# Fast matrix products for the keys and values of a linear attention, and a re-ordered beginning and end, in a four-layer hybrid kernel on one core

## The chip, the core and the metric

The kernel runs on one core of one Trainium2 chip. A core has a matmul engine (TensorE, PE in the profile; its weight loads are shown apart as PEld), VectorE (DVE), ScalarE (ACT), GpSimd (POOL) and SyncE (SP), each with its own in-order queue of instructions, and DMA queues that are fed by some of them. Data lie in HBM, are brought to SBUF (128 partitions), and matmul results land in PSUM banks of 128 x 512 f32. The metric is device time in microseconds for one execution.

## What is computed

The input x has 8 batches of 512 tokens with 256 features, all in f32. Four layers follow each other, each on the layer-normed x and added to x:

```python
x = x + linear_attention(layernorm(x))    # "a" in the names
x = x + ffn(layernorm(x))                 # "f"
x = x + attention(layernorm(x))           # "n", 16 heads of 64
x = x + ffn(layernorm(x))                 # "g", the same weights as "f"
```

The linear attention, whose keys and values the change is about, is

```python
Q = l2norm(x @ W_q.T); K = l2norm(x @ W_k.T); V = x @ W_v.T
global_feat = sum over tokens of (K * V) / 512
return Q * global_feat
```

The feed-forward layer mixes each token with the one before it (`xr = mu_r*x + (1-mu_r)*x_prev`, `xk` likewise), and returns `sigmoid(xr @ W_r.T) * (relu(xk @ W_k.T)**2 @ W_v.T)`. The softmax of the attention runs over the query axis.

## The kernel before

**The work.** Batches go through the layers in a software pipeline. The attention is done in 64 pairs of heads (8 batches x 8 pairs, numbered g). Two pairs at a time make one period: scores (`sc`, L1095), a row maximum on VectorE (`nm`, L1100), exponentials on ScalarE (`e`, L1111), values scaled by the sums' reciprocals on GpSimd (`vs`, L1128), and context (`cx`, L1148). Everything else (the linear attention and feed-forward layer of later batches, projections, the output projection `y`, the last feed-forward of earlier batches) is put between these blocks as filling.

**The order.** It is written out when the program is built. Each piece of filling is a generator that yields steps (engine, cost, earliest start), and a small planner (`Order`) keeps a clock for each engine, picks the next step by due time and readiness, and emits it. `until` runs what is due, `fill` adds more up to a share of TensorE's time that `total` hands out evenly. A table `CHOICES` has one entry for each period: an addition to the share, a slack, and a number that shuffles the ranks. On the chip each engine runs its instructions in just that order, and waits on semaphores.

**Seven products.** The head projections, the attention's values from the second batch on and the feed-forward keys from the third batch on are computed as 2 x 2 block matrices with seven products in place of eight (`seven`). It needs sums of weight blocks (made once, `sums_of_weights`), sums of row blocks (made for each batch on GpSimd; `sums_of_rows`, and in `keys` for the feed-forward), and additions behind the products: `begin` copies the first product out of PSUM, `join` and further additions on VectorE combine the rest (L883, L893, L903). Products 1 and 2 share a PSUM bank, 7 and 4, and 5 and 3: the second of each can begin when the result of the first has been used. The products are emitted in the order 1, 6, 7, 2, 5, 4, 3.

**The linear attention** (`linear`): for each half of a batch (256 tokens) the rows are normalized and transposed (the first three batches with TensorE, `normed_t`; the others by a DMA transpose, `normed_dma`). Then for each tile of 128 tokens two matmuls with 512 columns give keys and values together in a bank (L672); ScalarE copies the values out (L678) and sums the squared keys (L679), VectorE multiplies both (L683), and after the inverse norm (`power`, GpSimd) adds the tiles up with the norm as a factor (L692, L694). `mean` sums over tokens with one matmul, `queries` and `front` do the rest and go on to the feed-forward layer.

**The beginning.** Weights and the x of the first two batches are asked for at the start, then `al`. The first two batches' fronts are planned until the second is due (`order.until(-1)`), and after it come the loads of the third and fourth batch and the third one's front. SP's queue holds these loads in the order of the code.

**The end.** The last batch's last feed-forward runs by halves: four matmuls for the output of a half (L440, `o_g`), one multiplication (L569) and one addition (L618) of 128x512 on VectorE, and one store of 256 KB (L1052).

Buffers: `sums`, the row sums of the feed-forward keys, is one tile for each of two sets of buffers (`buffers(own)`, named sumsFalse and sumsTrue); `cpool` holds the contexts of 8 pairs.

Of the kernel before, what the change touches and what calls it, by code (L numbers as in the profile page):

```python
# [8 lines left out]
F32 = mybir.dt.float32  # L9
U16 = mybir.dt.uint16  # L10
AF = mybir.ActivationFunctionType
# [19 lines left out]
PAIRS, BANKS = 3, 2  # L31
X_LANDS = (4.1, 8.5, 12.0)
# [6 lines left out]
    (-4, 2, 90203), (0, 0, 43155), (0, 2, 0), (-2, 2, 77416), (1, 0, 8249), (-2, 1, 93964),  # L39
    (0, 0, 0), (-6, 1, 43070), (-2, 0, 51517), (-2, 2, 70093), (-2, 2, 81842), (-1, 2, 0),  # L40
    (1, 0, 13647), (6, 0, 84141), (1, 0, 16079), (4, 1, 90125), (-6, 0, 25271), (0, -1, 56854),
    (-2, 2, 47130), (0, -1, 47424), (0, 1, 8929), (4, 0, 14836), (-6, 0, 64258), (4, 2, 13478),
    (-1, 1, 84848), (2, 2, 74886), (1, 2, 58853), (4, 2, 96692), (6, 0, 82127), (4, 0, 41997),
    (0, 0, 0), (-1, -1, 26368), (6, 0, 83164), (0, 0, 0),
# [192 lines left out]
def kernel(ctx: ExitStack, tc: tile.TileContext, a: dict, out: bass.AP):  # L237
# [21 lines left out]
    cpool = ctx.enter_context(tc.tile_pool(name="cpool", bufs=8))  # L259
# [70 lines left out]
    def buffers(own):  # L330

        if own not in sets:
            s = {
                n: one.tile([P, 2, 512], F32, tag=f"{n}{own}", name=f"{n}{own}")
                for n in ("xn", "xr", "xk")
            }

            s["ka"], s["r"] = s["xn"], s["xk"]
            s["sums"] = one.tile([P, 3, HS], F32, tag=f"sums{own}", name=f"sums{own}")
            sets[own] = s  # L340
        return sets[own]

    def buffers_linear(b):

        if b < 2:
            return buffers(b == 1)
        if "linear" not in sets:
            n = {n: one.tile([P, 2, 512], F32, tag=f"{n}l", name=f"{n}l") for n in ("xn", "xr")}  # L350
            sets["linear"] = {"xn": n["xn"], "xk": n["xn"], "ka": n["xn"], "xr": n["xr"], "r": n["xr"]}
        return sets["linear"]

# [8 lines left out]
    def normed(src, name, s, h, ready, early=False):  # L362
# [7 lines left out]
        xn, rstd = tiles(s["xn"], h), small.tile([P, 2], F32, tag="rstd", name=f"rstd_{name}_{h}")  # L370
        if early:

            ready = yield "G", 1.05, ready
            nc.gpsimd.tensor_scalar(rstd, mv[:, :, 1], LN_EPS, 1.0, ALU.add, ALU.mult)
            nc.gpsimd.tensor_tensor(rstd, rstd, neg_half[:, :2], ALU.pow)
            ready = yield "V", 0.75, ready
            for u in range(2):
                nc.vector.tensor_scalar(
                    xn[:, u, :], src[:, 2 * h + u, :], mv[:, u, 0:1], rstd[:, u : u + 1],
                    ALU.subtract, ALU.mult,  # L380
                )
        else:

            shift = small.tile([P, 2], F32, tag="shift", name=f"shift_{name}_{h}")
            ready = yield "G", 1.4, ready
            nc.gpsimd.tensor_scalar(shift, mv[:, :, 0], -1.0, None, ALU.mult)
            nc.gpsimd.tensor_scalar(rstd, mv[:, :, 1], LN_EPS, 1.0, ALU.add, ALU.mult)
            nc.gpsimd.tensor_tensor(rstd, rstd, neg_half[:, :2], ALU.pow)
            nc.gpsimd.tensor_tensor(shift, shift, rstd, ALU.mult)
            ready = yield "A", 1.0, ready  # L390
            for u in range(2):
                nc.scalar.activation(
                    xn[:, u, :], src[:, 2 * h + u, :], AF.Identity,
                    bias=shift[:, u : u + 1], scale=rstd[:, u : u + 1],
                )
# [136 lines left out]
    def ffn(xb, name, s, h, ready, add_on, by_dma, due):  # L532
# [32 lines left out]
        order.give()  # L565
        ready = yield "T", BANK, squared, -1, mark
# [5 lines left out]

    def keys(name, s, ready):
# [3 lines left out]
        t = s["sums"]  # L577
        yield "G", 0.0, 0.0, -1, "sums_f"
        for dst, x0, x1 in (
            (t[:, 1, :], b22, b12), (b12, b12, b11), (t[:, 0, :], b22, b12),  # L580
            (t[:, 2, :], b21, t[:, 0, :]),
        ):
            ready = yield "G", 0.8, ready
            nc.gpsimd.tensor_tensor(dst, x0, x1, ALU.subtract)
        order.marks[name, "t"] = ready
        lhs = blocks_of_weights(fk, blocks["sums_f"], split_pairs, 0)
        rhs = [b11, b21, b22, t[:, 2, :], b12, t[:, 0, :], t[:, 1, :]]
# [18 lines left out]
        def through(h, ready):  # L606
            for f in (AF.Relu, AF.Square):
# [43 lines left out]
    def linear(b, h):  # L651
# [3 lines left out]
        xt, kv = chunks(s["xr"], h), tiles(s["ka"], h)  # L655
# [9 lines left out]
        order.marks[f"a{b}", h] = ready  # L665
        ss = small.tile([P, 2], F32, tag="ss", name=f"ssk_{b}_{h}")
        arrived = ready
        for u in range(2):
# [8 lines left out]
            vs = two.tile([P, D], F32, tag="av", name=f"av_{b}_{h}_{u}")  # L677
            nc.scalar.copy(vs, ps[:, D:])  # L678
            nc.scalar.activation(kv[:, u, :], ps[:, :D], AF.Square, accum_out=ss[:, u : u + 1])  # L679
            if u == 1:  # L680
                order.add(queries(b, h), *due_of(b))
            ready = yield "V", 0.35, ready
            nc.vector.tensor_mul(kv[:, u, :], ps[:, :D], vs)  # L683
            order.give()
        rn = small.tile([P, 2], F32, tag="rn", name=f"rnk_{b}_{h}")
# [11 lines left out]
        if both(f"a{b}"):  # L697
            order.add(mean(b, ready), *due_of(b))

# [94 lines left out]
    }  # L794
    blocks["sums_f"] = const.tile([P, 4, P], F32, tag="sums_f", name="sums_f")
# [243 lines left out]
    def tail(b, h, ready, due):  # L1039
# [9 lines left out]
        )  # L1049
        ts = slice(2 * h, 2 * h + 2)  # L1050
# [136 lines left out]
    add_front(1)  # L1187
    order.until(-1)
    al = weight("al", [P, NP, D], nc.sync)
    load_x(2)  # L1190
    load_x(3)
    add_front(2)
# [21 lines left out]
    total += 2 * FAST - 13 * FAST / 2  # L1214
# [76 lines left out]
```

## Time and profile before

| | |
|---|---|
| median of 3 runs | 1146.74 us (1146.02 to 1146.79) |
| the profiled execution | 1146.73 us, its span 1144.8 us |
| TensorE busy | 1125.2 us, 6994 records |
| VectorE, ScalarE, GpSimd busy | 806.0, 679.5, 478.9 us |
| granted TensorE clock | 1.0 |

A line of the profile's groups has the source line, engine, operation, output and inputs by the program's names, the shape (for a matmul partitions x columns of the weights, then the output), the count, then the busy time and the mean duration of one in nanoseconds, then idle time before it. Each f32 matmul shows as two records. Matmuls are pipelined, and a record's end is modelled: the mean of one is longer than the distance to the next.

```profile
L1111 ACT ACTIVATE e<-sc,nm 128x512 f32<-128x512 f32 x512 | 347.1, 690 | 123.1 <-DVE nm L1100 123.1
L1100 DVE TENSOR_REDUCE nm<-sc 128x2 f32<-128x1024 f32 x256 | 308.9, 1218 | 69.3 <-PE sc L1095 68.6
L672 PE MATMUL kv<-wkv,xrl 128*128 128x512 f32 x96 | 44.9, 595 | 0.0
L931 PE MATMUL m_qk<-xta,aq 128*128 128x256 f32 x124 | 38.8, 394 | 0.0
```

The third line is the work that the change rewrites: the keys and values of six batches, 48 matmuls of 512 columns. The fourth is one of the block products that the kernel already has, with 256 columns.

### The profile page before, as it was taken

Reading aid. Unit: us, or ns where it says so; the run is one execution under the profiler, and the core shown is the slowest. Engines: PE = TensorE matmul, PEld = TensorE weight load, DVE = VectorE, ACT = ScalarE, POOL = GpSimd, SP = SyncE. Lnnn points to the kernel's source line nnn. Section 1 sums busy time; section 2 is a strip of 40 time slices with the busy share of each in tenths; the row PEclk is TensorE's granted clock in tenths of the full one; section 3 lists DMA queues with packets and bytes.
Section 4 is the critical chain, followed back from the end, with each engine's and each line's share of the span. In section 5 each row is a group of like instructions: output and inputs, shape, how many; then the busy total and the mean of one; then the engine's idle time right before and its main releaser. Section 6 shows DMA issues by size and latency. Waiting matters only on the chain. (4 is left out here: it accounts for less than half of the span.)

```text
span 1144.8 us, 19233 instructions
## 1 busy us (share of the span) xinstructions
PE 1125.2 (98%) x6994; PEld 699.2 (61%) x6994; DVE 806.0 (70%) x1474; ACT 679.5 (59%) x1789; POOL 478.9 (42%) x760
## 2 busy tenths in 40 slices
PE   7999999999999999999999999999999999999998
PEld 4645456656556567666656555766656756665556
DVE  5775777667777767767677777777677777667754
ACT  3546756467663864655655676466574566645653
POOL 4455263224712484217542267343553442523201
PEclk9999999999999999999999999999999999999999
DMA  8000000000001110012100111010200110001001
GB/s 298 1 1 1 1 19 19 10 11 11 19 11 38 29 28 10 10 37 38 20 10 11 37 32 25 10 47 10 29 19 1 22 35 2 19 19 20 1 2 37
DMA packets 61182, 28.64 MB, mean 25 GB/s; under 512 B 51456, under 2 KB 59648, under 8 KB 60576
## 3 DMA queue, kind: packets, MB, share of 16 engines
q1 hardware_dynamic: 59936, 25.70, 9.2%
q8 instruction: 56, 0.92, 0.3%
q10 hardware_dynamic: 864, 1.05, 0.3%
q0 software_dynamic: 288, 0.67, 0.2%
q14 instruction: 38, 0.31, 0.1%
HBM read 10.63 MB, written 4.19 MB: 13 GB/s over the span
## 5 line engine op out<-in xcount | busy, mean ns | idle before, releaser
L1111 ACT ACTIVATE e<-sc,nm 128x512 f32<-128x512 f32 x512 | 347.1, 690 | 123.1 <-DVE nm L1100 123.1
L1100 DVE TENSOR_REDUCE nm<-sc 128x2 f32<-128x1024 f32 x256 | 308.9, 1218 | 69.3 <-PE sc L1095 68.6
L1095 PE MATMUL sc<-qk 64*64 64x512 f32 x2048 | 270.1, 594 | 2.6 <-DVE qk L903 1.7
L1148 PE MATMUL cx<-e,vs 64*64 64x512 f32 x2048 | 269.1, 589 | 0.0
L1128 POOL TENSOR_TENSOR vs<-v,rs 128x256 f32<-128x256 f32 x128 | 79.0, 618 | 381.8 <-DVE rs L1124 353.6
L1148 PEld LDWEIGHTS cx<-e,vs 64*64 64x64 f32 x2048 | 87.2, 133 | 136.9 <-issue 114.5
L1095 PEld LDWEIGHTS sc<-qk 64*64 64x64 f32 x2048 | 76.1, 132 | 138.9 <-issue 86.8
L440 PE MATMUL y<-al,ctx 128*128 128x256 f32 x512 | 116.4, 380 | 0.4 <-ACT prev_f L517 0.4
L440 PEld LDWEIGHTS y<-al,ctx 128*128 128x128 f32 x512 | 96.6, 190 | 17.5 <-ACT e L1111 3.2
L1111 ACT ACTIVATION_READ_ACCUMULATOR e<-sc,nm 128x1 f32 x512 | 105.3, 206 | 0.0
L939 ACT ACTIVATE qk<-m_qk,bias 128x256 f32<-128x256 f32 x124 | 52.2, 475 | 51.7 <-PE m_qk L931 50.1
L1156 DVE TENSOR_TENSOR ctx<-cx,ctx 128x512 f32<-128x512 f32 x64 | 44.3, 692 | 47.3 <-ACT ctx L1155 46.3
L947 DVE SCALAR_TENSOR_TENSOR qk<-m_qk,dbias,qk 128x256 f32<-128x256 f32 x124 | 54.1, 478 | 18.3 <-PE m_qk L931 17.7
L1031 DVE TENSOR_TENSOR x<-y,x 128x512 f32<-128x512 f32 x32 | 22.0, 687 | 35.5 <-PE y L440 35.4
L672 PE MATMUL kv<-wkv,xrl 128*128 128x512 f32 x96 | 44.9, 595 | 0.0
L1155 ACT COPY ctx<-cx 128x512 f32<-128x512 f32 x64 | 37.4, 585 | 10.4 <-PE cx L1148 10.4
L931 PE MATMUL m_qk<-xta,sums_q 128*128 128x256 f32 x124 | 38.0, 388 | 1.0 <-DVE qk L893 0.9
L931 PE MATMUL m_qk<-xta,aq 128*128 128x256 f32 x124 | 38.8, 394 | 0.0
L931 PE MATMUL m_qk<-xts,aq 128*128 128x256 f32 x124 | 37.4, 383 | 0.4 <-DVE qk L883 0.4
L931 PE MATMUL m_qk<-xta,ak 128*128 128x256 f32 x124 | 36.9, 379 | 0.0
L931 PE MATMUL m_qk<-xts,ak 128*128 128x256 f32 x124 | 36.9, 379 | 0.0
L931 PE MATMUL m_qk<-xta,sums_k 128*128 128x256 f32 x124 | 36.9, 379 | 0.0
(303 smaller groups left out, 1941.8 us busy)
## 6 DMA issues: line engine op xcount, KB each, us to landing
out<-x SPq DMA_DIRECT2D x16, 256.0 KB, 2.1
x<-in_x SPq DMA_DIRECT2D x6, 512.0 KB, 4.0
aq<-in_aq SPq DMA_DIRECT2D x1, 1024.0 KB, 8.1
ak<-in_ak SPq DMA_DIRECT2D x1, 1024.0 KB, 10.1
av<-in_av SPq DMA_DIRECT2D x1, 1024.0 KB, 12.1
al<-in_al SPq DMA_DIRECT2D x1, 1024.0 KB, 14.5
x<-in_x ACTq DMA_DIRECT2D x4, 128.0 KB, 4.0
x<-in_x SPq DMA_DIRECT2D x4, 128.0 KB, 4.1
```

The costliest lines, as they stand in the source:

```text
L440: nc.tensor.matmul(ps[:, u * D : (u + 1) * D], lhsT=lhs[i][:, u * P : (u + 1) * P], rhs=rhs[i], start=(i == 0), stop=(i == n - 1),)
L672: nc.tensor.matmul(ps, lhsT=xt[:, kc, u * P : (u + 1) * P], rhs=wkv[:, kc, :], start=(kc == 0), stop=(kc == KC - 1),)
L931: nc.tensor.matmul(ps[:, w * HS : (w + 1) * HS], lhsT=lhs[w][n - 1], rhs=block_of_rows(b, n), start=start and w == 0, stop=True, skip_grou ...
L939: nc.scalar.activation(dst[:, w, :], ps[:, w, :], AF.Identity, bias=bias[:, w, p : p + 1])
L947: nc.vector.scalar_tensor_tensor(dst[:, w, :], ps[:, w, :], dbias[:, w, p // 2 : p // 2 + 1], part[:, w, :], ALU.add, ALU.add,)
L1095: nc.tensor.matmul(ps[m * HD : (m + 1) * HD, j, :], lhsT=kt[hs, keys], rhs=qt[hs, :], start=True, stop=True,)
L1100: nc.vector.tensor_reduce(nm, ps, AX.X, ALU.max, negate=True)
L1111: nc.scalar.activation(e[:, j, :], ps[:, j, :], AF.Exp, bias=nm[:, j : j + 1], accum_out=sums[g, h][:, c % 2, j : j + 1],)
L1128: nc.gpsimd.tensor_tensor(vs, vh[b, p // 4][:, 2 * h : 2 * h + 2, cols].rearrange("p t (j d) -> p t j d", j=2), rs.unsqueeze(3).to_broadca ...
L1148: nc.tensor.matmul(cx[m][j * HD : (j + 1) * HD, :], lhsT=vsc[g, c // 2][ks, c % 2, j, :], rhs=es[g, c][ks, j, :], start=(c == 0), stop=(c ...
L1155: nc.scalar.copy(ct, cx[0])
L1156: nc.vector.tensor_tensor(ct, cx[1], ct, ALU.add)
```

## The change

Keys and values of batches 3 to 8 (b > 1) go through `seven`: the blocks are the two halves of the tokens by the two chunks of features for the rows, and the two chunks of features by keys and values for the weights. `wkv` gets its weight sums once the first two batches have used it plainly (its one block is overwritten by the fourth sum). The squares are summed from SBUF after the products, and halves and tiles are added on VectorE.

The row sums of the feed-forward keys and of the new products share one buffer (`sums_of`), whose users are put in a row by a mark each. `cpool` has 7 buffers. In the first two batches the values are copied into a buffer of the set, not into one of their own.

```diff
-    cpool = ctx.enter_context(tc.tile_pool(name="cpool", bufs=8))
+    cpool = ctx.enter_context(tc.tile_pool(name="cpool", bufs=7))
...
+    def sums_of(blocks_of, t1, ready):
+        n = len(users)
+        users.append(n)
+        (b11, b12), (b21, b22) = blocks_of
+        yield "G", 0.0, 0.0, -1, ("t", n - 1) if n else None
+        t = one.tile([P, 4, HS], F32, tag="sums", name=f"sums_{n}")
+        t1 = t[:, 3, :] if t1 is None else t1
+        for dst, x0, x1 in (
+            (t[:, 1, :], b22, b12), (t1, b12, b11), (t[:, 0, :], b22, t1),
+            (t[:, 2, :], b21, t[:, 0, :]),
+        ):
+            ready = yield "G", 0.75, ready
+            nc.gpsimd.tensor_tensor(dst, x0, x1, ALU.subtract)
+        return [b11, b21, b22, t[:, 2, :], t1, t[:, 0, :], t[:, 1, :]], t, n, ready
...
+        if b > 1:
+            if both(f"a{b}"):
+                order.add(keys_values(b, s, ready), *due_of(b))
+            return
...
+    def keys_values(b, s, ready):
+        xt = [chunks(s["xr"], h) for h in range(2)]
+        yield "G", 0.0, 0.0, -1, "sums_kv"
+        lhs, t, user, ready = yield from sums_of(
+            [[xt[h][:, kc, :] for h in range(2)] for kc in range(KC)], None, ready
+        )
+        order.marks["kv", b, "t"] = ready
+        rhs = blocks_of_weights(wkv, blocks["sums_kv"], split_values, 0)
+        k, v = ([tiles(s[n], h) for h in range(2)] for n in ("xn", "v"))
+        def mul(ps, n, start):
+            for u in range(2):
+                nc.tensor.matmul(
+                    ps[:, u * D : (u + 1) * D], lhsT=lhs[n - 1][:, u * P : (u + 1) * P],
+                    rhs=rhs[n - 1], start=start and u == 0, stop=True, skip_group_check=True,
+                )
+        def begin(ps, dst, ready):
+            ready = yield "A", 0.62, ready
+            nc.scalar.copy(dst, ps)
+            return ready
+        def join(ps, dst, part, ready, first):
+            ready = yield "V", 0.62, ready
+            nc.vector.tensor_tensor(dst, ps, part, ALU.add)
+            return ready
+        def through(h, ready):
...
+            for u in range(2):
+                nc.scalar.activation(
+                    t[:, 2, :], k[h][:, u, :], AF.Square, accum_out=ss[:, u : u + 1]
+                )
...
+            for u in range(2):
+                nc.vector.scalar_tensor_tensor(
+                    k[h][:, u, :], k[h][:, u, :], rn[:, u : u + 1], v[h][:, u, :],
+                    ALU.mult, ALU.mult,
+                )
+            if both(f"kv{b}"):
...
+                nc.vector.tensor_tensor(k[0], k[0], k[1], ALU.add)
+                ready = yield "V", 0.4, ready
+                means[b] = k[0][:, 0, :]
+                nc.vector.tensor_tensor(means[b], means[b], k[0][:, 1, :], ALU.add)
+                order.add(mean(b, ready), *due_of(b))
+        yield from seven(f"kv_{b}", ("kv", b, "t"), mul, [k, v], begin, join, 1.0, through)
```

The third batch's load and front are put ahead of `order.until(-1)`, so that its work can be planned among that of the first two, and its load ahead of `al` on SP's queue. The output of the last batch's last feed-forward is computed, multiplied, added and stored by tiles of 128 tokens.

```diff
+    load_x(2)
+    asked[2] = WEIGHTS_LAND - X_LANDS[2]
+    add_front(2)
+    order.add(sums_of_weights(wkv, "sums_kv", split_values, "plain_kv"), 0)
     order.until(-1)
     al = weight("al", [P, NP, D], nc.sync)
-    load_x(2)
     load_x(3)
-    add_front(2)
...
+    def last_rows(xb, name, h, ka, r, ready):
...
+        for u in range(2):
+            done = yield "T", BANK / 2, ready
+            ps = bank(f"o_{name}_{h}_{u}")[:, :D]
+            for kc in range(KC):
+                nc.tensor.matmul(
+                    ps, lhsT=ka[:, kc, u * P : (u + 1) * P], rhs=fv[:, kc, :],
+                    start=(kc == 0), stop=(kc == KC - 1),
+                )
+            ends.append((ps, done))
+        for u, (ps, done) in enumerate(ends):
+            ru = r[:, u * D : (u + 1) * D]
+            ready = yield "V", 0.36, done
+            nc.vector.scalar_tensor_tensor(ru, ru, 1.0, ps, ALU.add, ALU.mult)
+            ready = yield "V", 0.36, ready
+            xt = xb[:, 2 * h + u, :]
+            nc.vector.tensor_tensor(xt, xt, ru, ALU.add)
+            nc.sync.dma_start(out=rows_out[:, 2 * h + u, :], in_=xt)
...
-    total += 2 * FAST - 13 * FAST / 2
+    total += 2 * FAST - 13 * FAST / 2 - 6 * FAST
```

All 34 entries of `CHOICES` are replaced by others, so the filling of every period is put together anew; no period keeps its order of instructions.

## Prediction

> **What bounds the kernel now.** I read first the page's busy times and its row of slices, then the list of what TensorE waited for, then the chain of waits and the timeline at the places where TensorE did wait.
>
> ```profile
> PE 1125.2 (98%) x6994; PEld 699.2 (61%) x6994; DVE 806.0 (70%) x1474; ACT 679.5 (59%) x1789; POOL 478.9 (42%) x760
> ...
> PE   7999999999999999999999999999999999999998
> ...
> PEclk9999999999999999999999999999999999999999
> ```
>
> TensorE (PE) is busy in all slices but the first and the last, at full granted clock; VectorE (DVE) comes next with 70%. So the span is TensorE's work plus what TensorE waits. A busy share doesn't show work at its peak, so I take the price of a product from start to start, in the chain of waits:
>
> ```profile
> 830.04 0.86 PE m_qk L931 x4
> 830.90 1.72 PE kv L672 x4
> 832.62 0.86 PE m_qk L931 x4
> ```
>
> Each f32 matmul leaves two records. Four records of 256 columns take 0.86 us, four of 512 take 1.72: a matmul costs 0.43 us at 256 columns and 0.86 at 512, and narrow ones lose nothing by being narrow. What TensorE waits for is short:
>
> ```profile
> PE tr_a L406 <- DVE xnFalse L378: 6.4, 1, 6.4
> PE sc L1095 <- DVE qk L903: 1.7, 4, 0.4
> PE sc L1095 <- ACT xnl L392: 0.9, 1, 0.9
> PE m_qk L931 <- DVE qk L893: 0.9, 2, 0.4
> PE kv L672 <- ACT xrTrue L659: 0.7, 1, 0.7
> PE v L1006 <- ACT xta L766: 0.7, 1, 0.7
> PE kv L672 <- DVE xnTrue L683: 0.6, 1, 0.6
> ...
> PE tr_f L406 <- DVE xnTrue L378: 0.4, 1, 0.4
> PE o_f L440 <- ACT xnFalse L560: 0.4, 1, 0.4
> PE m_k_g L591 <- DVE xnTrue L893: 0.3, 1, 0.3
> ```
>
> The first 6.4 us are the load of x and its normalization, which the change leaves alone. The rest is some 8 us in all. A change can therefore gain what it takes from TensorE's work, plus a part of these waits, and it can lose by new ones.
>
> **The seven products.** For each of the six batches from the third on, keys and values took 4 token tiles x 2 chunks = 8 matmuls of 512 columns; now 7 products x 2 matmuls of 256. So 8 x 0.86 = 6.88 us become 14 x 0.43 = 6.02 us, and six batches give **-5.2 us** on the engine that sets the end. Bounds: -5.2, if the new matmuls run like m_qk, and -4.2, if one of seven products in each batch (0.86 us) pays 0.17 us of change-over as the widest of the small hitches in the trace (0.11 to 0.23) do.
>
> Other engines: VectorE adds per batch six 128x512 additions (0.69, from L903) and one 128x256 (0.42), and drops four at L683 (0.42): +2.9 us, in all +17 (806 to 823). ScalarE drops 24 copies of 0.37 and adds 12 of 0.59: -2. GpSimd (POOL) adds 24 + 4 subtractions or additions of 0.73 (the rows of L584): +20 (479 to 499). I cost these at nothing: they run beside TensorE on engines that stand idle for 28% or more of the span. Without that cover the 0.69 us of each of the 36 new wide additions would be the price.
>
> In the changed instruction order the new chains have room. From the fifth product to the third, between which VectorE must add, other matmuls of 1.7 us or more stand in all six batches, where 0.2 + 0.69 is needed. The shared row-sum buffer has 19 users; the shortest stretch of TensorE's work from one user's last product to the next one's first is 20.7 us, and the four subtractions take 2.9. The context pool cut from 8 to 7 buffers: a buffer's last reader on TensorE is at least 15 us ahead of its next writer. All three cost nothing.
>
> [...]
>
> **The third batch's front.** Its load moves on SP's queue ahead of the 1 MB of `al`, and it was issued at 10.2 us and landed 16.9 us later, at about 27; now it can only land earlier. VectorE, where its statistics stand in front of the first feed-forward's mixing, reaches them at about 31 us (the multiplications at L683 that stand ahead of them end at 30.5 in the trace of before). `al` lands later by the 0.5 MB, and is read first after 100 us. Its work then fills TensorE's early waits. In the changed order a transpose of the third batch and the mean stand ahead of o_f (0.4), two value products ahead of the second batch's transpose (0.4), a query product ahead of the last kv (0.6). The waits of kv for its copy (0.7) and of v for xta (0.7) stay as they are. **-1.4 us**; bounds 0, if the GpSimd chain of the new front delays the others as much as it fills, and -3.0, all six early waits.
>
> **The end.**
>
> ```profile
> 1138.36 1.89 PE L440 MATMUL o_g<-fv,xnFalse 128*128 128x256 f32 x8
> 1140.36 0.69 DVE L569 SCALAR_TENSOR_TENSOR xkFalse<-xkFalse,o_g 128x512 f32<-128x512 f32 x1 [2.04 <-PE o_g L440]
> 1141.08 0.69 DVE L618 TENSOR_TENSOR x<-x,xkFalse 128x512 f32<-128x512 f32 x1
> ```
>
> Behind the last matmul two operations of 0.69 us stand in a row, then a store. Cut by token tiles, the first tile's two (0.42 each, the 128x256 row) end as the second's begin, and only 0.84 of 1.38 us is left: **-0.5 us**. Four stores of 128 KB replace two; each issue takes 0.37 us on SP, and the tiles come 0.86 apart. The store's landing (2.1 us at 256 KB) I leave at 2.1. Bounds -0.9 and -0.2.
>
> **What the new order costs.** All waits move, since the planner's table of choices is replaced. Three kinds can be counted in both orders.
>
> ```profile
> 160.10 0.59 PE L931 MATMUL m_qk<-xta,sums_k 128*128 128x256 f32 x2
> 160.73 0.69 DVE L903 TENSOR_TENSOR qk<-m_qk,qk 128x512 f32<-128x512 f32 x1 [0.29 <-PE m_qk L931]
> ...
> 321.64 0.59 PE L591 MATMUL m_k_g<-sumsTrue,fk 128*128 128x256 f32 x2
> ...
> 322.32 0.70 PE L591 MATMUL m_k_g<-xkTrue,sums_f 128*128 128x256 f32 x2
> ```
>
> *Scores straight behind their projection.* The last product's matmuls are fed until 160.53; VectorE's addition ends at 161.42, and the scores begin at 161.57: 0.94 us more than the 0.1 of an undisturbed entry. With one matmul between (0.43) the excess is 0.51, with two 0.1. Before: one place with none between, three with one, three with two: 0.94 + 1.53 + 0.3 = 2.8. Changed: four with none, three with two: 3.8 + 0.3 = 4.1. **+1.3 us**, bounds 0 and +2.5 (one more 0.3 at each of four, where feed-forward mixing is queued on VectorE ahead of the addition).
>
> *Feed-forward keys in a row.* The third product waits for an addition behind the fifth: it starts 0.68 us after the fourth, not 0.43: 0.25 lost. That happened once; in the changed order nine of thirteen chains stand so. **+2.0 us**, bounds +0.8 and +2.8.
>
> *Values in a row.* Four chains with 0.86 between lost 0.16 to 0.23 each; none does now: **-0.7 us**, bounds -0.8 and 0.
>
> The other waits after the start, some 2.4 us in the list, I take as unchanged (0 to twice as much).
>
> Sum: -5.2 - 1.4 - 0.5 + 1.3 + 2.0 - 0.7 = -4.5 us. The profiled execution took 1146.73 us, 1144.8 of it span, 1.9 around it, and is within 0.01 us of the median of the runs. So 1140.3 + 1.9 = **1142.2 us**.
>
> [...]
>
> **Rivals.**
>
> *The redrawn order sheds waits.* The counts above are of places; where VectorE is early, a place costs less, and two thirds of the +3.3 may not come. For it: 8 us of waits in 1145 show what this planner can do. Against it: nine chains stand where the trace has the 0.25 us. Price: -5.2 - 3.0 - 0.5 + 1.1 - 0.7 = -8.3, or 1138.4 us.
>
> *Given back.* VectorE, at 72%, brings its additions late in some five more places at 0.6 us (as at 386.20 to 386.81), and the front fills nothing: -4.5 + 3.0 + 1.4 = -0.1, 1146.6 us, no change. For it: the changed order puts feed-forward mixing between the additions of three tight projections. Against: idle time of 28%.
>
> *Slower: VectorE becomes what chains wait for.* The 36 wide additions and 28 GpSimd sums land where scores, projections and feed-forward all want VectorE. It decides from about twelve late additions of 0.6 us beyond the counted ones: -4.5 + 12 x 0.6 = +2.7, 1149.4 us. For it: 17 us more in an in-order queue. Against: the new chains have 1.7 us or more of cover each.
>
> *The front doesn't move.* If the third batch's x were late, VectorE would stand still for it at 31 us; at 27 it has landed in either order. The term would be 0: 1143.6 us, inside the forecast.
>
> **How the numbers follow.** Forecast 0.60 (1139.7 to 1144.4, the front's rival in it), shedding 0.15, given back 0.16, slower 0.09. A measurement of this kernel tells a change from none at about 0.2%, 2.3 us: faster 0.75, same 0.16, slower 0.09. The sums of low and high ends, taken half each since they won't all fall together, are about 4 us to either side; the given-back case lies above, so the range is 1138.0 to 1146.0.
>
> **What would show it.** TensorE's records of the kv products 36 us in all, in groups of 0.86 between other work; waits of sc for L1012 near 4; m_k waiting for VectorE nine times at 0.2 to 0.3; two operations of 0.42 behind the last matmul. It would be wrong if waits of vs or e for GpSimd or VectorE stretched the attention blocks (13.9 us now), or if the kv matmuls came apart at more than 0.43.

## The result and the profile after

The changed kernel takes 1148.47 us (median of 20, 1147.99 to 1149.8), the one before 1146.76 (median of 20, 1145.65 to 1147.77): ratio 1.0016, 95% interval 1.0009 to 1.0022. It is 1.7 us slower where 4.5 us less were forecast. In some of the runs below the executions fall into two groups 2.4 to 3.1 us apart, and there the text says how many took which time. The page's first lines for the changed kernel:

```profile
PE 1121.5 (98%) x7066; PEld 714.3 (62%) x7066; DVE 828.4 (72%) x1496; ACT 682.0 (59%) x1777; POOL 501.5 (44%) x788
...
PEclk9999999999999999999999999999999999999999
```

GpSimd did what was forecast (479 to 502 us, 499 forecast), and ScalarE is nearly unchanged. VectorE rose by 22.4 us, from 806.0 to 828.4, where the counted operations at their clean durations gave 17: the new operations took longer than their price. The products, in the chain of waits of the changed kernel (start, duration, what):

```profile
834.01 0.86 PE m_qk L1040 x4
834.87 0.86 PE m_kv L763 x4
```

Four records of 256 columns take 0.86 us, as m_qk does. From the list of what TensorE waited for (total, times, longest), behind the load of x:

```profile
PE sc L1206 <- DVE qk L1012: 2.0, 3, 0.9
PE sc L1206 <- DVE prev_g L485: 1.8, 2, 0.9
PE tr_a L429 <- DVE xkFalse L594: 1.2, 1, 1.2
...
PE cx L1259 <- DVE prev_f L483: 1.0, 1, 1.0
PE q L463 <- DVE xrTrue L546: 0.9, 1, 0.9
PE m_qk L1040 <- DVE qk L1002: 0.8, 1, 0.8
```

All six of these are waits for VectorE, and most are new. To see where the time went I add up the same account for each run: for every TensorE record, the distance to the next one's start less its price (0.213 us for 256 columns, 0.427 for 512; 0.107 for the 64x64 matmuls of scores and context with 512 columns, of which 16 take 1.72). The step out of a block is counted inside it. The parts sum to the span:

```
us                           before    after       e2       e8      e16       e5
first record starts            6.38     6.23     6.46     6.13     6.30     6.41
slow records up to 12 us       2.67     1.65     2.67     2.93     2.05     2.04
other waits before scores      5.97     8.34     7.94     8.33     8.29     6.53
inside attention blocks       12.00    13.60    13.28    13.25    14.32    13.09
at the step into a block       6.55     8.48     8.43     8.50     8.41     8.50
in the filling                20.65    23.07    20.41    21.96    21.58    20.76
behind the last matmul         4.75     4.07     4.08     4.08     4.09     4.08
TensorE's work              1085.87  1080.75  1080.75  1080.75  1080.75  1080.75
span                        1144.83  1146.19  1144.01  1145.92  1145.78  1142.15
from the first scores on    1073.50  1065.12  1062.09  1063.68  1064.28  1062.32
```

Work fell by 5.1 us and the end by 0.7. Waits before the first scores grew by 2.4, inside blocks by 1.6, at the steps into them by 1.9, in the filling by 2.4. The second row differs from execution to execution of one start (1.65 to 3.24 over the runs of the changed start); below, runs are compared from the first scores on where the start isn't the question.

The end, in the timeline (start, duration, engine, line, operation):

```profile
1141.53 0.42 DVE L615 SCALAR_TENSOR_TENSOR xkFalse<-xkFalse,o_g 128x256 f32<-128x256 f32 x1 [1.77 <-PE o_g L607]
1141.98 0.42 DVE L618 TENSOR_TENSOR x<-x,xkFalse 128x256 f32<-128x256 f32 x1
1142.33 0.41 DVE L615 SCALAR_TENSOR_TENSOR xkFalse<-xkFalse,o_g 128x256 f32<-128x256 f32 x1
```

The second tile's multiplication (third line) follows the first tile's two operations of 0.42 us; one more addition ends at 1143.2.

The new waits, at two places. The timeline at 699 us, VectorE, GpSimd and TensorE of the changed kernel:

```profile
699.78 1.90 DVE L792 SCALAR_TENSOR_TENSOR xnl<-xnl,rnk,vl 128x256 f32<-128x256 f32 x2
701.60 0.68 DVE L1002 TENSOR_TENSOR qk<-m_qk,qk 128x512 f32<-128x512 f32 x1
...
700.08 1.38 POOL L451 COPY xta<-xkFalse 128x1024 uint16<-128x1024 uint16 x1
...
702.33 0.70 PE L1040 MATMUL m_qk<-xta,sums_q 128*128 128x256 f32 x2 [0.79 <-DVE qk L1002]
```

The pair of new multiplications L792, which nobody waits for here, stands ahead of the addition L1002, which TensorE waits for; and beside GpSimd's copy the two take 1.90 us; the shortest of the 24 took 0.45 us. And at the start:

```profile
39.96 1.80 DVE L852 SCALAR_TENSOR_TENSOR xkTrue<-xkTrue,rnq,gf 128x256 f32<-128x256 f32 x2 [0.95 <-ACT xnl L415]
41.69 0.67 DVE L594 SCALAR_TENSOR_TENSOR xkFalse<-xkFalse,o_f 128x512 f32<-128x512 f32 x1
...
39.89 0.73 POOL L929 TENSOR_TENSOR sums_kv<-sums_kv,wkv 128x256 f32<-128x256 f32 x1
...
42.51 0.63 PE L429 MATMUL tr_a<-ident,xnl 128*128 128x128 f32 x4 [1.25 <-DVE xkFalse L594]
```

L852 is stretched beside the new weight sums of keys and values (L929, three in a row to 42.36), L594 frees its PSUM bank late, and a transpose of the moved front waits 1.25 us for a bank.

### The profile page after: what moved, and what is told of

Read it like the earlier page. It is cut to its first block, busy times and chain, and to the rows that moved or that the text cites. A ratio compares the mean times of both kernels' runs of the same rounds, so it can differ in the third digit from the quotient of the medians.

```text
span 1146.2 us, 19444 instructions
## 1 busy us (share of the span) xinstructions
PE 1121.5 (98%) x7066; PEld 714.3 (62%) x7066; DVE 828.4 (72%) x1496; ACT 682.0 (59%) x1777; POOL 501.5 (44%) x788
## 5 line engine op out<-in xcount | busy, mean ns | idle before, releaser
L1140 DVE TENSOR_TENSOR x<-y,x 128x512 f32<-128x512 f32 x32 | 22.1, 690 | 42.8 <-PE y L463 42.7
L540 ACT ACTIVATE prev_g<-xrTrue,omu 128x255 f32<-128x255 f32 x56 | 26.7, 477 | 15.3 <-DVE qk L992 3.7
```

What stands on the lines that cost most here:

```text
L540: nc.scalar.activation(ps[:, kc, 1:], xr[:, kc, : HS - 1], AF.Identity, scale=omu[:, i, kc : kc + 1])
```

## The experiments

Each of the labels e2 to e8 has the changed kernel's own instruction order, but for what its text says; times are medians of 11 beside the kernel before on the same chip. It took 1146.7 to 1146.9 each time, so the runs can be set beside the changed kernel's 1148.47 to some 0.2 us. The ratios are estimates with a 95% interval and need not equal the quotients of the medians.

**e1: the end alone, on the kernel before.** The edit is `last_rows` and its call, as in the change.

```diff
+        if add_on is nc.vector and name[0] == "g":
+            return (yield from last_rows(xb, name, h, ka, r, squared))
```

> The kernel before with one part of the change, the last feed-forward's end by token tiles; the order of all else is that of before. The prediction's term: 0.5 us less, 1146.2 (1145.8 to 1146.5), and in the trace the last matmul is followed by two operations of about 0.42 us where two of 0.69 stood, so the time from the last matmul record to the end of the span falls from 4.75 to about 4.1 us. Rival: four stores instead of two land later and give it back, 1146.6 to 1147.0.

1146.50 us, ratio 0.9994 (0.9985 to 1.0003): the time can't tell it from no change. The account can: the row behind the last matmul falls from 4.75 to 4.07 us, and the stretch from the first scores on from 1073.50 to 1073.21, with 0.4 more inside the blocks.

**e2: the new VectorE work behind the products taken off.**

```diff
-    k[h][:, u, :], k[h][:, u, :], rn[:, u : u + 1], v[h][:, u, :],
+    k[h][:, u, :16], k[h][:, u, :16], rn[:, u : u + 1], v[h][:, u, :16],
...
-nc.vector.tensor_tensor(k[0], k[0], k[1], ALU.add)
+nc.vector.tensor_tensor(k[0][:, :, :16], k[0][:, :, :16], k[1][:, :, :16], ALU.add)
...
```

> The changed kernel in its own instruction order on every engine. Only the operations behind the new products are made narrow: the 24 multiplications by the row norm and by v (L792) work on 16 of their 256 columns, the six wide and six half-wide additions behind them (L800, L803) on 16 too. What is left out is the product k*v outside these columns, so the mean row isn't the reference's. VectorE loses some 25 us of 828. Theory A (late VectorE: the new operations with both inputs in SBUF, stretched beside GpSimd, make VectorE late for additions and maxima that TensorE awaits): 2.5 us below the changed kernel's 1148.5, that is 1146.0, between 1144.5 and 1147.0; the wait of m_qk at 702.3, that of q near 725 and those of cx near 632 and 777 shrink. Theory B (the redrawn order alone makes the new waits, whatever the side work costs): 1148.0 to 1149.0, the waits stay where they are.

1145.73 us, ratio 0.9988 (0.9979 to 0.9997): 2.7 us below the changed kernel, as theory A had it. From the first scores on it is 3.0 us shorter, 2.7 of it in the filling. VectorE at 699 us of this run:

```profile
699.60 0.37 DVE L792 SCALAR_TENSOR_TENSOR xnl<-xnl,rnk,vl 128x16 f32<-128x16 f32 x2
700.53 0.69 DVE L1002 TENSOR_TENSOR qk<-m_qk,qk 128x512 f32<-128x512 f32 x1 [0.56 <-PE m_qk L1040]
```

Now VectorE waits for TensorE (0.56), not TensorE for it. The gaps of 0.48 at 282, 0.96 at 701 and 1.08 at 724 are gone and the block at 565 is back to 13.98 us. But the waits of cx at 632 and 780, which I had put to the same cause, stayed (blocks of 15.13 and 15.59): that part of theory A fell.

**e3, e4, e5: GpSimd's new work taken off.** e3 makes the row sums of keys and values narrow (first lines), e4 the weight sums (last lines), e5 both and e2's cut.

```diff
+            if few:
+                dst, x0, x1 = dst[:, :16], b22[:, :16], b12[:, :16]
             nc.gpsimd.tensor_tensor(dst, x0, x1, ALU.subtract)
...
+            if tag == "sums_kv":
+                dst, x0, x1 = dst[:, :, :16], a11[:, :, :16], a12[:, :, :16]
             nc.gpsimd.tensor_tensor(dst, x0, x1, op)
...
```

> The changed kernel in its own order. The 24 GpSimd subtractions that make the row sums of keys and values (four for each of six batches) work on 16 of 256 columns, and the products take a block of the rows itself where they took a sum. What is left out is the row sums, so keys and values from the third batch on aren't the reference's. GpSimd loses some 16 us of 501. Theory A (contention: GpSimd's new work stretches VectorE's operations and delays the chains): 1 us below the changed kernel, 1147.5, between 1146.5 and 1148.0. Theory B (order): 1148.0 to 1149.0.

1148.70 us, ratio 1.0018 (1.0009 to 1.0027): nothing. 16 us of GpSimd's new work cost no time; theory A's share for it fell.

> The changed kernel in its own order. The four GpSimd operations at about 40 us that make the sums of the weights of keys and values (L929) work on 16 of 256 columns, and the products take the weights themselves where they took a sum; left out are these sums, so keys and values from the third batch on aren't the reference's. Theory A for the front (the multiplication and addition of the first feed-forward, L852 and L594, come late by GpSimd beside them, and the transpose of the second batch waits 1.25 us for the bank): 1.0 us below the changed kernel, 1147.5, between 1147.0 and 1148.0, and the first scores at 80.0 instead of 81.1. Theory B (the bank is late by the order of VectorE's queue): the wait at 42.5 stays, 1148.2 to 1148.8.

1147.08 us, ratio 1.0008 (0.9999 to 1.0017), so 1.4 below the changed kernel, in six of eleven executions; the other five took 1149.1 to 1149.9 (see the last section). The profiled execution is one of these five: its first scores begin at 82.4 us, so the expected 80.0 isn't shown there (e5's begin at 79.8). L852 is back to 0.88 us in its timeline, L594 follows at once, and the 1.25 us wait is gone:

```profile
40.52 0.88 DVE L852 SCALAR_TENSOR_TENSOR xkTrue<-xkTrue,rnq,gf 128x256 f32<-128x256 f32 x2 [0.94 <-POOL rnq L692]
```

> The changed kernel in its own order with the three cuts of the other runs together: the narrow VectorE operations behind the new products, the narrow row sums and the narrow weight sums. Left out are the sums of rows and weights of keys and values and k*v outside 16 columns, so linear attention from the third batch on isn't the reference's. Theory A: the cuts add up, 4.5 us below the changed kernel, 1144.0, between 1142.5 and 1145.5, so below the kernel before by 2.7. Theory B (order): less than 1 us below, 1147.5 to 1148.7, and the waits that grew from before to after stay for most of their length.

1144.01 us, ratio 0.9981 (0.9972 to 0.9990): 4.5 below the changed kernel. The cuts add up. This is again the upper end of six executions of eleven; the other five took 1146.0 to 1146.7. So even with all its new side work gone the change brings 2.8 us over the kernel before, not 4.5, and in the longer executions some 0.4.

**e6, e16: the same work, later in VectorE's queue.** The multiplications and additions are kept back until so many later steps of VectorE have been issued: e6 at four places, e16 only in b = 6.

```diff
+LATER = {
+    (3, "first"): 2, (3, "second"): 1,
+    (5, "second"): 3, (5, "wide"): 2, (5, "half"): 1,
+    (6, "first"): 3, (6, "wide"): 1,
+}
...
+            put(products, LATER.get((b, "second" if second else "first"), 0))
```

> The changed kernel, all of its computation, with seven VectorE instructions groups issued a little later in VectorE's queue and nothing else moved: in the third linear batch counted from 1 (b = 3) the two pairs of multiplications L792 behind the addition of L1140, in b = 5 one pair and L800, L803 behind L1140 and the first maximum of L1211, in b = 6 one pair behind the additions L1002, L1056, L1012 and L800 behind the mixing L546. Theory A (at these four places an operation that nobody awaits stands, stretched, ahead of one that TensorE awaits): the waits of 0.48 us at 282, 0.4 at 565, 0.96 at 701 and 1.08 at 724 go, 2.2 us below the changed kernel: 1146.3, between 1145.6 and 1147.2. Theory B (what counts is the amount of VectorE's work, not its place): less than 0.5 below, 1148.0 to 1148.7.

1148.33 us, ratio 1.0015 (1.0006 to 1.0024): theory B. The filling lost 1.4 us of waits, the blocks won 1.2.

> The changed kernel, all of its computation, with two groups of VectorE instructions issued later: in b = 6 the first pair of multiplications L792 behind L1002, L1056 and L1012, and L800 behind the mixing L546. Theory A (place): the wait of 0.96 us at 701 goes, that of 1.08 at 724 falls to some 0.4, and at most 0.6 comes back in the block behind the first: 1.0 us below the changed kernel's 1148.5, that is 1147.5, between 1146.8 and 1148.0. Theory B (amount: VectorE is full there and what is taken away comes back): 1148.2 to 1148.8. Neither expects it below the kernel before.

1148.45 us, ratio 1.0016 (1.0007 to 1.0025), inside B's range. But the six executions with a mean clock of 0.999 are its six longest, and the other five have a median of 1147.92, inside A's, so the times don't decide between the two. In the profiled execution, one of the five, the stretch from the first scores on is 0.84 us shorter than the changed kernel's (filling -1.5, blocks +0.7). Where the wait went can be read in VectorE's timeline of e16:

```profile
703.59 1.34 DVE L824 SCALAR_TENSOR_TENSOR xnl<-xnl,rnk,vl 128x256 f32<-128x256 f32 x2
704.86 0.69 DVE L514 TENSOR_TENSOR prev_g<-edge_g,omu 128x2 f32<-128x2 f32 x1
705.58 0.87 DVE L575 SCALAR_TENSOR_TENSOR xkTrue<-xrTrue,mu,prev_g 128x256 f32<-128x256 f32 x2
706.37 1.22 DVE L1249 TENSOR_REDUCE nm<-sc 128x2 f32<-128x1024 f32 x1
```

The products no longer wait for the multiplications (here L824), but the first maximum of the next block does, behind them and the mixing: that block takes 14.53 us, not 13.89. Moving work inside a full queue moves the wait; here the trace won half of it.

**e7: later, and three weight sums early.** e6, with three of the four L929 operations issued at 11 us, behind the second batch's inverse deviation.

```diff
+            if name == "a1" and both("sums_early"):
+                (a11, a21), (a12, a22) = [split_values(wkv[:, kc, :]) for kc in range(KC)]
+                s1, s2, s4 = (blocks["sums_kv"][:, i, :].unsqueeze(1) for i in range(3))
...
-            nc.gpsimd.tensor_tensor(dst, x0, x1, op)
+            if tag != "sums_kv" or dst is s3:
+                nc.gpsimd.tensor_tensor(dst, x0, x1, op)
```

> The kernel with the later multiplications, and three of the four weight sums of keys and values (L929, three GpSimd operations of 0.75 us) issued at 11 us, where GpSimd stands idle until 15, instead of at 35 to 42; the fourth, which writes into the weights themselves, stays. All of the computation. Theory A (front): the first feed-forward's multiplication L852 takes some 1.1 us instead of 1.8, the transpose of the second batch waits 0.4 instead of 1.25, and 1.0 us more is gained: 1145.3, between 1144.5 and 1146.3, below the kernel before. Rival: the early sums stretch the normalization of the second batch (L402) and the gain is given back: 1146.0 to 1147.0.

The median is 1149.94 us, ratio 1.0018 (1.0010 to 1.0027), from two groups: three of eleven executions took 1147.0 to 1147.3, six 1149.9 to 1150.4, and two 1148.1 and 1148.2. That is outside both ranges. The transpose's wait did shrink, to 0.3 us. In the profiled execution, one of the longer ones, the granted clock fell to 0.50 from 49.9 to 53.3 us; the gain can't be had reliably.

**e8: GpSimd's old row sums narrow, VectorE whole.**

```diff
+            dst, x0, x1 = t[:, 1, :16], b22[:, :16], b12[:, :16]
             nc.gpsimd.tensor_tensor(dst, x0, x1, ALU.subtract)
...
```

> The changed kernel in its own order, VectorE's work whole, and GpSimd's other row sums made narrow: the subtractions for the feed-forward keys (L374, 13 x 4) and for the attention rows (L948) work on 16 columns, and the products take the blocks where they took sums. Left out are these sums, so feed-forward keys, queries, keys and values of the attention aren't the reference's. These are GpSimd's neighbours of L792, L800 and L803 at 282, 565 and partly at 724, not at 701. Theory A1 (what makes VectorE late is the stretch beside GpSimd): the waits at 282 and 565 go and that at 724 shrinks, 1.3 us below the changed kernel: 1147.2, between 1146.4 and 1147.8; L792's median falls from 0.85 to below 0.65 us. Theory A2 (it is the plain load of the new operations): the waits stay, 1148.0 to 1148.8.

1147.92 us, ratio 1.0010 (1.0001 to 1.0019). The median lies between the two ranges, and two executions took 1149.8 and 1150.1; from the first scores on the profiled execution is 1.43 us shorter than the changed kernel's, as A1 had it. At 280 us four multiplications stand ahead of the addition L1140 that frees a bank. In the changed kernel's timeline, with the first of its four neighbours on GpSimd:

```profile
279.37 3.08 DVE L792 SCALAR_TENSOR_TENSOR xnl<-xnl,rnk,vl 128x256 f32<-128x256 f32 x4
...
279.54 0.91 POOL L374 TENSOR_TENSOR sums<-xkTrue 128x256 f32<-128x256 f32 x1 [1.46 <-DVE xkTrue L546]
```

and in e8's, where the line numbers are a few higher:

```profile
280.54 1.67 DVE L797 SCALAR_TENSOR_TENSOR xnl<-xnl,rnk,vl 128x256 f32<-128x256 f32 x4
...
280.70 1.58 POOL L377 TENSOR_TENSOR sums<-xkTrue 128x16 f32<-128x16 f32 x4 [1.46 <-DVE xkTrue L551]
```

3.08 us became 1.67 with VectorE's work unchanged, and the gap of 0.48 at 282 and the wait in the block at 565 went. The median of L792 fell from 846 to 476 ns. So about half of e2's 3.0 us is stretch by these GpSimd neighbours (the products of e8 don't wait for the row sums either, but no wait of TensorE for GpSimd was in the changed kernel's list); at 701, where the neighbour is a copy that e8 leaves alone, the wait stayed at 0.96.

**e9, e10, e11: other orders.** Only `CHOICES` is replaced, here the first entries of e9's:

```diff
-    (-2, 0, 86105), (2, 1, 88627), (1, 2, 0), (2, 2, 33867), (1, 2, 0), (0, 0, 0), (-4, 1, 69171),
+    (-2, 0, 86105), (-2, 1, 66392), (-2, 2, 0), (2, 2, 13335), (1, 0, 0), (1, -1, 0), (-4, 1, 0),
```

> The changed kernel with another table of choices, from a random walk of some 12,000 tables that starts at its own and keeps what shortens the planner's own clock: that clock says 1132.0 where the changed kernel's own table gives 1134.4 (and the kernel before 1136.9). The chip is 14.1 us above that clock in the changed kernel and 9.8 in the one before. Theory S (the change makes waits the planner doesn't see, in whatever order): 14 us above, 1146.1, between 1145 and 1147.2. Theory L (the changed kernel's order was unlucky): some 10 us above, 1142, between 1141 and 1144.

> The same with a second table, found by a walk of its own: the planner's clock says 1132.5. Theory S: 1146.6, between 1145.4 and 1147.7. Theory L: 1142.5, between 1141.5 and 1144.5.

> The control: the kernel before with a table from an equally long walk; the planner's clock says 1134.8, 2.1 below its own table's. Theory S: 9.8 above, 1144.6, between 1143.5 and 1145.7, so the two kernels stay apart from the planner's gain by about 4 us. Theory L: the distance scatters by several us from table to table in this kernel too, 1142 to 1149.

e9 1147.92 (1.0013, 1.0004 to 1.0021), e10 1148.55 (1.0015, 1.0006 to 1.0024), e11 1153.38 us (median of 5; 1.0069, 1.0056 to 1.0083). The distances from the planner's clock are 15.9, 16.1 and 18.6 us, after 14.1 and 9.8 for the own tables. Neither theory held: three orders of the changed kernel lie within 0.6 us, but a table that the planner takes for better made the kernel before 6.7 us slower, 4.0 of it in one wait at 777 us. Theory S came nearer for the changed kernel, with medians 0.7 and 0.9 us above its ranges, and theory L's scatter nearer for the control. The planner's clock doesn't rank orders to some us, and how much of the kernel before's 1146.8 is a table that suits the chip stays open.

**e12: the third batch's front put back**, one execution.

```diff
-    load_x(2)
-    asked[2] = WEIGHTS_LAND - X_LANDS[2]
-    add_front(2)
     order.add(sums_of_weights(wkv, "sums_kv", split_values, "plain_kv"), 0)
     order.until(-1)
     al = weight("al", [P, NP, D], nc.sync)
+    load_x(2)
     load_x(3)
+    add_front(2)
```

> One part of the change undone: the third batch's load and front begin behind the first stretch, as in the kernel before; all else of the changed kernel. Since the table of choices fits the other order, the whole is far slower (the planner's clock says 1221) and only the start is read: what TensorE waits before the first scores. The prediction's term says the moved front fills 1.4 us of waits, so here 10 + 1.4 = 11.4 us are lost before the first scores. Rival (the moved front fills nothing, its GpSimd and VectorE work delays the first feed-forward): 8.5 to 9.0, as in the kernel before (8.64).

1233.8 us as a whole. The row of other waits before the scores is 4.05 us, against 8.34 with the front moved: the moved front fills nothing, it costs. Three of the waits that it should have filled (o_f 0.4, kv 0.6, tr_f 0.4 in the list of before) are gone here too, where it stands behind; the first two are gone in the changed kernel, but new ones came. (The expectation's totals are the second and third row together: 8.64 before, 9.99 changed, and 6.42 here, below both of its values.) TensorE's timeline runs without a wait where the changed kernel had 1.25 us:

```profile
39.35 1.89 PE L574 MATMUL k_f<-xkFalse,fk 128*128 128x256 f32 x8
41.08 1.89 PE L463 MATMUL r_f<-fr,xrFalse 128*128 128x256 f32 x8
```

The two starts don't hold the same work (first scores at 70.4 and 81.1 us), so 4.3 us is not a clean price. What the later part of e12 pays for the third batch can't be read, since its filling is put together by a table that doesn't fit; the 1.25 us wait, which e4 takes away by itself, is the clean part.

**e13, e14, e15: maxima ahead of mixing.** Where feed-forward mixing stands directly ahead of a maximum in VectorE's queue, the maximum goes first: the mixing is kept back until VectorE's next step. e15 adds e16's edit.

```diff
-            first_column(ps, name, h, i)
-            for kc in range(KC):
+            def mixing(ps=ps, i=i, dst=dst):
+                first_column(ps, name, h, i)
+                for kc in range(KC):
...
+            late.append((at, mixing))
```

> The changed kernel, all of its computation; at the four places where feed-forward mixing (L485 or L483 and L546) stands directly ahead of a maximum of scores (L1211) in VectorE's queue, the maximum goes first. These are the block at 632 (15.14 us instead of 13.9), that at 780 (15.52) and two more. Theory A (order of the queue): the two blocks shorten to 14.5 or less and 1.5 us are gained, 1147.0, between 1146.3 and 1147.8. Theory B (VectorE is full there, the next maximum waits instead): 1148.0 to 1148.8.

> The kernel before with the end by token tiles and the same rule for maxima, which changes two places there: the block at 420 (14.92 us) and one of the two next to it. Theory A: 0.5 us for the end and 0.8 for the blocks, 1145.5, between 1144.7 and 1146.2. Theory B: no more than the end brought alone, 1146.2 to 1146.8.

> The changed kernel with the maxima first and, in b = 6 alone, the first pair of multiplications L792 behind L1002, L1056 and L1012, and L800 behind the mixing L546: the places of the earlier run where the wait that was taken away (0.96 at 701, 1.08 at 724) came back in the block at 704 behind mixing, which now stands behind the maximum. Theory A: 1.2 us below the run with maxima first alone, 1145.8, between 1145.0 and 1146.7, so not slower than the kernel before. Theory B: less than 0.5 below that run.

e13 1149.72 us (1.0022, 1.0013 to 1.0031), e14 1147.87 (1.0011, 1.0002 to 1.0020), e15 1147.99 (1.0008, 0.9999 to 1.0016). e13 and e14 are slower than both theories had them. Theory A fell: the block at 632 stayed at 15.12 us in e13, and in e14 the block at 421 grew from 14.92 to 18.28. There cx waits 1.62 us for the mixing (`cx <- DVE xkTrue`), and a stretch of halved clock from 425.2 to 428.6 us lies in the block as well; the profiled execution is one of three that took 1150.4 to 1150.8 with a mean clock of 0.999, the other eight took 1147.4 to 1147.9 with 1.0. What cx waits for at these places is not the maximum but the mixing (at 632 `cx <- DVE prev_f`), which reads a PSUM bank that cx takes next. That reading of the wait is an argument from the names in the list; no run took the bank away. Against e13, e15 is 1.7 us faster, more than its theory asked, so at the two places of b = 6 the queue's order is worth something. It gave 0.84 us without the maxima's edit too (e16, from the first scores on), and against the changed kernel e15 is 0.99 us shorter by the same measure.

No version with the whole computation was measurably faster than the kernel before.

## Why the prediction was wrong

**Seven products, -5.2:** right. TensorE's work fell by 5.12 us, and m_kv runs like m_qk, 0.86 us for four records.

**The end, -0.5:** right; 0.68 in the account.

**What the new order costs, +1.3 + 2.0 - 0.7:** the sums nearly held. The step into blocks cost 1.9 more (+1.3 forecast); the gaps of over 0.1 us in feed-forward keys went from 0.69 to 2.70 (+2.0 forecast); those of values from 0.78 to 0.37 (-0.4, -0.7 forecast). That the keys fit so well is partly luck: eight chains, not nine, lost 0.11 to 0.36 each, 1.3 us more than before, and most of the rest is one wait of 0.56 at 740 us, for an addition that I had not counted.

**The third batch's front, -1.4:** this step failed first. I bounded it by 0, "if the GpSimd chain of the new front delays the others as much as it fills", and looked at when x lands and at which work would stand ahead of which wait, not at the queues of VectorE and GpSimd there. The row before the scores grew by 2.4. The change had put a second thing into the start, the four weight sums on GpSimd, which I had costed at nothing with the others: beside them L852 took 1.80 us instead of 0.88, and the bank came late. e4 and e12 show it: without these sums the 1.25 us wait is gone, without the moved front the row is 4.05; and with all new side work narrow (e5) it is 6.53, so 1.8 of the 2.4 are that work's. A term that moves three engines' work into a stretch with waits needed a bound on the loss side too.

**"I cost these at nothing":** this failed second, by some 3 us (e2: 2.7 by the medians, 3.0 from the first scores on). The idle share, 28%, was of the whole span. The filling is where it isn't idle: at 699, 280, 562 and 722 us the new operations stood in an unbroken queue ahead of one that TensorE awaited. The trace of before has this stretch beside GpSimd, an addition of 1.54 us where the same line takes 0.69 at the end, and I gave it no term; e8 shows that half of the cost is this stretch. "The other waits unchanged" fell with it.

```profile
46.71 1.26 POOL L784 TENSOR_TENSOR x<-x,lb 128x512 f32<-128x512 f32 x1 [1.20 <-ACT xnFalse L392]
46.98 1.54 DVE L618 TENSOR_TENSOR x<-x,xkFalse 128x512 f32<-128x512 f32 x1
```

**The rivals:** "Slower: VectorE becomes what chains wait for" named the mechanism and 1149.4; it asked for twelve late additions and there were some four places, the rest came from the front. "Given back" came nearest: it had the front filling nothing and some five late additions for 3.0 us, which is what e2 took off; it lacked the front's loss. "The front doesn't move" had 0 for the term; it was worse than that.

The sum of the misses: front 3.8 (-1.4 to +2.4), unforeseen waits in filling and blocks 2.4 (their 4.0 less what the keys and values explain, 1.6), scores 0.6, values 0.3, products 0.1, end -0.2, a luckier start of the profiled execution -1.2, and 0.5 from it to the median: 6.3, for 6.2 between -4.5 and +1.7.

## What to carry to other kernels

An engine's idle share hides new work only where the work lands: look at the queue of the stretch that it goes to, and at what is awaited behind it there. Price new VectorE operations like L792 beside GpSimd by the stretched row (here 0.85 us, its median), not the clean one (0.45, its shortest). And moving work into early waits needs every engine's queue of that stretch, not only the arrival of the data.

## What the runs showed of the hardware

**The stretch beside GpSimd is a wait, not a rate.** With 256 columns a multiplication L792 took 454 to 1504 ns (median 846), with 16 columns still 205 to 1302 ns; the wide addition L800 684 to 1636, with 16 columns of each tile 184 to 1178 (median 640). Even the two-column L514 above took 0.69 us, where 0.16 is usual. VectorE additions that read a PSUM tile (L775, 683 to 693 ns) weren't touched, though GpSimd worked beside eight of the twelve. In the changed kernel's trace the fourteen L792 of 832 to 1504 ns each began 0.05 to 0.31 us after an operation of GpSimd, and ended 0.22 to 0.28 us after its end; beside the other ten, of 454 to 481 ns, none had begun in the 0.32 us before.

**In some executions the granted clock was halved for 3.4 us behind a stretch with little TensorE work.** In e4's profiled execution it was, from 48.7 to 52.1 us; in e7's from 49.9 to 53.3, in e14's from 425.2 to 428.6, and in e12's six times behind its long waits, for 3.4 to 20.5 us (mean clock 0.979). The windows of e4 (stretch and its length, then busy time and count for PE, PEld, DVE, ACT and POOL; the third number from the right is the granted clock):

```profile
48.00:50.00 2.00, 1.47 (x2) 0.69 (x3) 1.93 (x6) 0.48 (x1) 2.00 (x3) 0.68 0.00 0
50.00:52.00 2.00, 2.00 (x4) 0.71 (x3) 0.74 (x1) 0.00 (x0) 1.73 (x4) 0.50 0.00 0
```

The executions of e4, e5, e7 and e14 come in two groups, 2.4 to 3.1 us apart by their medians; all 20 of the changed kernel have a mean clock of 1.0. A mean clock of 0.999 alone doesn't tell the groups apart: three of e4's six quick executions have it, and those of the kernel before that have it were the shorter ones (35 with a median of 1146.5, 93 without it 1147.0). In the eighteen traces the rows of the granted clock up to the last matmul last whole multiples of 3.41 us (1136.64 us in the changed kernel's, 333 of them; 1133.22 in that of before, 332). By the prices of the table the 3.41 us ahead of a halved stretch held 1.36 us of TensorE's work in e4 and e7, 1.26 in e14 and 0 to 1.28 in e12. The emptiest 3.41 us, counted along the rows, held 1.66 in the changed kernel's profiled execution and 1.79 in that of before, and there the clock stayed at 1.0. Little work ahead isn't the whole of it: some stretches with 1.27 to 1.33 had no halved one behind them. Whether the place of these stretches on the waits near 47 us (in e4 TensorE has 0.9 us of transposes between 46.2 and 48.5 us) makes the two groups is not shown, since only one execution of each run has a profile.

**The first matmuls (from 6 to 9 or 12 us) ran at half pace for a time that varied.** In the kernel before, matmul records of 512 columns (kv) start 0.85 us apart from 8.4 to 11.0 us and 0.43 apart from 11.6 on. 1.65 to 3.24 us are lost so over the runs of the changed start. The windows show a granted clock of 1.00 there, but the traces have no row of the granted clock before 9.3 (changed kernel) to 12.4 us (e7), and half the time from the first matmul to that first row (1.52 and 3.04 us) is the loss to within 0.25 us in all eighteen traces. Two profiles differ there by up to 1.6 us with the same start.
